# Transformer block on one core: row sums taken with the last projection, squares and normalizing on ScalarE, and modulation of two tiles at once

## The chip, the cores and the metric

The kernel runs on one core of one Trainium2 chip. The metric is the device time of one execution in microseconds (us), the median of several runs of the same program. A profile of one execution, taken by the hardware profiler, goes with it. Engine names are those of the profile: PE (TensorE, matmuls), DVE (VectorE), ACT (ScalarE), POOL (GpSimd), SP (SyncE, which only issues transfers here).

## The reference

```python
h = _layernorm(x, axis=-1) * (1 + ca) + sa
x = x + ga * attention(h)          # 16 heads, softmax over the query axis
h = _layernorm(x, axis=-1) * (1 + cb) + sb
x = x + gb * ffn(h)                # fp4 blocks: w_down(silu(w_gate h) * (w_up h))
```

x is (2, 2048, 256) in float32. The six rows ca to gb come from a small product of c with wmod and are the same for all rows of a batch. In the feed-forward part (256 to 704 and back) the activations, h and the hidden product, are rounded to a grid of fp4 values in blocks of 16 with a scale of their own; the weights as well. The layer norm is `(x - mean) / sqrt(var + 1e-5)` over the 256 numbers of a row.

## The kernel before

**Tiles.** A tile is 128 rows of x, one row per partition, 256 numbers long. A batch has 16 tiles, in four groups of four. The attention of both batches takes the greater part of the time, and the feed-forward of the first batch is spread between the attention steps of the second. For the second (last) batch nothing is left to hide behind, so that its last projection and its feed-forward stand at the end, as a tail with functions of its own.

**Order of work.** Every piece of work is a Python generator (a chain) with a due time. The class `Order` plans: it keeps a clock for each engine, estimates each operation, and emits whatever can start first, due times deciding between candidates. What comes out is one fixed list of instructions for each engine, executed in that order; an instruction that has to wait holds back all behind it on its engine. Buffers are counted as "rooms": three places `s` of two PSUM banks each, two single banks `o`, five `e` buffers, two `ln`, and so on. A chain that takes a room waits until an earlier owner gives it back.

**The tail, as the change finds it.** `project_last` multiplies the attention output of the last four heads with the output projection, tile by tile, into PSUM: tiles 0 to 3, 4 to 7 and 8 to 11 into `s` places (`op_0`, `op_4`, `op_8`), tiles 12, 13 and 14, 15 into the two `o` banks (`op_12`, `op_14`). `projected` brings the result into x. For tiles 0 to 7 VectorE adds it to x. For tiles 8 to 15 (`ADD_X = 2`, in groups of four) x itself has been added in PSUM, by one more matmul with the identity, and ScalarE or VectorE copies the sum out. `ffn_stats` takes mean and variance of each row with `bn_stats` and `bn_aggr` (in `ln_stats`), then an inverse root by three Newton steps on tiny operands; it handles tile 0, tiles 1 to 3, and then four tiles at a time. `tail_norm` makes h with two VectorE operations per tile, `(x - mean) * (1 + cb)` and `h * r + sb`, for tile 0, tile 1, and then pairs, and quantizes the result (`quantize`, ten small or large steps, of which `MAGIC` goes to ScalarE and the last product to GpSimd or VectorE). `tail` then does one tile: transpose of h (`hq`, into an `o` bank), a copy by ScalarE, the two products `pg` and `pu` (8 rows of the trace each), silu on ScalarE, product and quantizing on VectorE (tile `e`), transpose (`h2t`), copy by ScalarE, and `dn`: x by the identity, then six products with the down weights. Tile 15 is done in two halves. In names below, `pg_3` is the product of tile 3, and so on.

Two things about `project_last` matter for the change: the matmul that writes a further part of a PSUM place waits until the part before it has been read, and `hq_0`, the first transpose of the tail, takes the `o` bank that `op_12` used.

Of the kernel before, what the change touches and what calls it, by code (L numbers as in the profile page):

```python
# [10 lines left out]
F32 = mybir.dt.float32  # L11
# [3 lines left out]
AF = mybir.ActivationFunctionType  # L15
ALU = mybir.AluOpType
# [4 lines left out]
P = 128  # L21
EPS = 1e-5
# [22 lines left out]
TAIL_MARGIN = 0.5  # L45
# [2 lines left out]

PROJECT_DUE = -0.5, 0.0, 0.2, 0.4
PROJECTED = (0, 4), (4, 4), (8, 4), (12, 2), (14, 2)  # L50
ADD_X = 2
NORM_DUE = -0.4, -0.2, 0.6
STATS_LEAD = 4
NORM_LEAD = 3.5
LAST_LEAD = 0.5
SPLIT = 1
# [54 lines left out]
class Order:  # L111
# [23 lines left out]
    def signal(self, key, of=1, early=0.0):  # L135

        n, t = self.counts.get(key, (0, 0.0))
        n, t = n + 1, max(t, self.chain.end - early)
        self.counts[key] = (n, t)
        if n == of:  # L140
            self.done[key] = t
        return n == of

    def give(self, name, n=1, place=0):
        for _ in range(n):
            heapq.heappush(self.rooms[name], (self.chain.end, place))
# [188 lines left out]
def adaln_block(  # L335
# [15 lines left out]
    B, N, D = x_in.shape  # L351
# [3 lines left out]
    I = w_gate.shape[0]  # L355
    KC = D // P
    NT = N // P
# [17 lines left out]
    T, V, A, G, S = (  # L375
        Queue(n, e)
        for n, e in (
            ("PE", nc.tensor),
            ("DVE", nc.vector),
            ("ACT", nc.scalar),  # L380
            ("POOL", nc.gpsimd),
            ("SP", nc.sync),
        )
# [4 lines left out]
            h=2, qm=2, h2=2, h2t=1, hqt=1, st=1, qs=3, ln=2,  # L388
# [4 lines left out]
    signal, give, due = order.signal, order.give, order.due  # L393

    const = ctx.enter_context(tc.tile_pool(name="const", bufs=1))
# [8 lines left out]
    vp = ctx.enter_context(tc.tile_pool(name="vp", bufs=5))  # L404
    w2 = ctx.enter_context(tc.tile_pool(name="w2", bufs=2))
    small = ctx.enter_context(tc.tile_pool(name="small", bufs=6))

    def banks(place, name):

        return ps_s.tile([P, 2, 512], F32, tag=f"s{place}", name=name)  # L410
# [7 lines left out]
    def either(first, second, margin):  # L418
        return Best(first, second, margin=COPY_MARGIN if margin is None else margin)

    def copy(dst, src, margin=None):
        return either(A.copy(dst, src), V.tensor_copy(dst, src), margin)

    def matmuls(dst, pairs, first=True):
        return [
            T.matmul(dst, lhsT=l, rhs=r, start=(first and k == 0), stop=(k == len(pairs) - 1))
            for k, (l, r) in enumerate(pairs)
        ]
# [22 lines left out]
    def x_tile(b, t):  # L451
        return xs[b, t // 4][:, t % 4, :]
# [6 lines left out]
    def mod(b, which):  # L459
        return mods[:, b, MODS.index(which), :]  # L460
# [31 lines left out]
    ident = const.tile([P, P], F32, tag="ident", name="ident")  # L492
# [78 lines left out]
        signal("mods")  # L571


    def ln_stats(x4, name, centre=False):


        n = x4.shape[1]
        yield Wait(take=["ln"])
        mv = small.tile([P, 4, 2], F32, tag="mv", name=f"mv{name}", bufs=2)
        for t in range(n):  # L580
            st = small.tile([P, 6], F32, tag="bst", name=f"st{name}_{t}")
            yield Free(V.bn_stats(st, x4[:, t, :]))
            yield V.bn_aggr(mv[:, t, :], st)
        v, r, e, c = (
            small.tile([P, 4], F32, tag=f"ln{i}", name=f"ln{i}{name}", bufs=2)[:, 0:n]
            for i in range(4)
        )
        yield V.tensor_scalar(v, mv[:, 0:n, 1], EPS, None, ALU.add)

        yield V.tensor_scalar(r.bitcast(U32), v.bitcast(U32), 1, None, ALU.logical_shift_right)  # L590
        yield V.tensor_scalar(
            r.bitcast(I32), r.bitcast(I32), -1.0, float(0x5F3759DF), ALU.mult, ALU.add
        )
        for i in range(3):
            yield V.tensor_tensor(e, r, r, ALU.mult)
            yield V.scalar_tensor_tensor(e, e, -0.5, v, ALU.mult, ALU.mult)
            if i < 2:
                yield V.scalar_tensor_tensor(r, e, 1.5, r, ALU.add, ALU.mult)
        yield V.scalar_tensor_tensor(e, e, 0.5, r, ALU.add, ALU.mult)
        yield V.tensor_tensor(r, r, e, ALU.add)  # L600
        if centre:
            return mv[:, :, 0], r
        yield V.scalar_tensor_tensor(c, mv[:, 0:n, 0], -1.0, r, ALU.mult, ALU.mult)
        return c, r

    def pool(*args, margin):
        if margin is None:
# [598 lines left out]
    def project_last(b, q, t, n):  # L1206

        g = t // 4
        room = "s" if n > 2 else "o"
        (place,) = yield Wait(  # L1210
            [("osb", b, q, g), ("wo", b, q), ("x", b, g)]
            + [("out", b, q - 1, t + j) for j in range(n)],
            [room],
        )
        name = f"op{b}_{q}_{t}"
        if room == "s":
            ps = banks(place, name)
        else:
            ps = ps_o.tile([P, 512], F32, tag="o", name=name).unsqueeze(1)
        taken = [1, 1, 2] if t == 0 else [2] * (n // 2)  # L1220
        for k, m in enumerate(taken):
            first = sum(taken[:k])
            part = ps[:, first // 2, first % 2 * D : (first % 2 + m) * D]
            for j in range(m):
                u = t + first + j
                pairs = [
                    (o_sb[b, 2 * q + c][:, u * P : (u + 1) * P], wos[b, q][:, c, :])
                    for c in range(2)
                ]
                if g >= ADD_X:  # L1230
                    pairs = [(ident, x_tile(b, u))] + pairs
                yield Free(matmuls(part[:, j * D : (j + 1) * D], pairs))
            order.add(
                projected(b, q, t + first, m, part, order.chain.end, (room, place, t, len(taken))),
                order.chain.due,
            )

    def projected(b, q, t, n, ps, ready, where):

        room, place, first, parts = where  # L1240
        order.chain.base = ready + order.CROSS
        x2 = xs[b, t // 4][:, t % 4 : t % 4 + n, :]
        ps = ps.rearrange("p (j d) -> p j d", d=D)
        if t // 4 >= ADD_X:
            yield copy(x2, ps, TAIL_MARGIN)
        else:
            yield V.tensor_tensor(x2, ps, x2, ALU.add)
        if signal(("projected", b, q, first), of=parts):
            give(room, place=place)
        for j in range(n):  # L1250
            signal(("out", b, q, t + j))

    def load_x(b, g):
        yield Wait(take=["x"])
# [3 lines left out]


    lns = {}  # L1260

    def lns_of(t):

        return t - t % 4 if t > 3 else min(t, 1)

    def ffn_stats(b, t, n):
        yield Wait([("out", b, NQUAD - 1, t + j) for j in range(n)])
        x4 = xs[b, t // 4][:, t % 4 : t % 4 + n, :]
        c, r = yield from ln_stats(x4, f"f{b}_{t}", centre=b == B - 1)
        for j in range(n):  # L1270
            lns[b, t + j] = (c, r, j, n)
        signal(("ln", b, t))
# [73 lines left out]
        give("h2t")  # L1346


    tails = {}

    def silu_table():
        yield Wait([("w", len(steps) - 1, 0)])
        yield A.activation(sig[:, :, 0], sig[:, :, 0], AF.Silu)
# [18 lines left out]
    def residual(ps, b, t):  # L1372
        return T.matmul(ps[:, 0:D], lhsT=ident, rhs=x_tile(b, t), start=True, stop=False)

    def tail_norm(b, t, n):

        margin = 0.0 if t < 2 else TAIL_MARGIN
        yield Wait([("ln", b, lns_of(t))], ["v"])
        w = vp.tile([P, 2, 2, D], F32, tag="v", name=f"w{b}_{t}")
        for j in range(n):  # L1380
            mean, r, k, of = lns[b, t + j]
            h, x = w[:, 0, j, :], x_tile(b, t + j)
            yield Free(
                V.scalar_tensor_tensor(
                    h, x, mean[:, k : k + 1], mod(b, "cb"), ALU.subtract, ALU.mult
                )
            )
            signal(("centred", b, t + j))
        for j in range(n):
            mean, r, k, of = lns[b, t + j]  # L1390
            h = w[:, 0, j, :]
            yield Wait([("centred", b, t + j)])
            yield Free(
                V.scalar_tensor_tensor(h, h, r[:, k : k + 1], mod(b, "sb"), ALU.mult, ALU.add)
            )
            if signal(("applied", b, t + j - k), of=of):
                give("ln")
        h, m = (w[:, i, 0:n].rearrange("p j d -> p (j d)") for i in range(2))
        yield from quantize(h, n * D // BLK, f"h{b}_{t}", m, margin)
        for j in range(n):  # L1400
            tails[b, t + j] = (w, j, n)
            signal(("normed", b, t + j))
# [138 lines left out]
    for b in range(B):  # L1541
# [28 lines left out]
        else:  # L1570
# [5 lines left out]
            for t in (0, 1, *range(2, NT, 2)):  # L1576
                if t < 4:
                    dues = d + NORM_DUE[(t + 1) // 2]
                else:
                    dues = d + t - STATS_LEAD  # L1580
                if t == lns_of(t):
                    add(ffn_stats(b, t, (1, 3)[t] if t < 4 else 4), dues)
                add(tail_norm(b, t, 1 if t < 2 else 2), dues if t < 4 else d + t - NORM_LEAD)
            for t in range(NT):
# [49 lines left out]
```

## Time and profile before

| | us |
|---|---|
| median of 3 runs | 1929.37 (1929.2 to 1930.44) |
| the profiled execution's own time | 1929.38 |
| its span in the trace | 1927.6 |
| PE busy | 1898.0 (98%) |
| DVE busy | 1711.0 (89%) |
| ACT busy | 1317.7 (68%) |
| POOL busy | 617.2 (32%) |
| first projection matmul of the tail | 1749.25 |
| first `pg` matmul of the tail | 1770.40 |
| last matmuls (`dn` of tile 15) | 1922.83 |

Times inside the trace count from the start of the span. The granted clock of PE was full. All operations are recorded by one helper, so that every row has the same line (L273), and one reads by the tile names. A duration in a row includes some overlap with the next row on the same engine: what an operation costs its queue is the distance from one start to the next. The trace shows each float32 matmul as two rows.

### The profile page before, as it was taken

The numbers are of one execution on the slowest core, as the hardware profiler recorded it, in microseconds if no ns is written. First come the engines' busy times: TensorE is split into PE (matmuls) and PEld (weight loads), VectorE is DVE, ScalarE is ACT, GpSimd is POOL, SyncE is SP. The second block draws the span as 40 slices with busy tenths as digits, with TensorE's granted clock in tenths as the row PEclk, the third lists the DMA queues.
The fourth block names the chain that finished last, engine by engine and source line by source line (L and its number), as shares of the span: only waits on it lengthen the run. The fifth ranks groups of instructions, "written<-read, shape, count | busy, mean of one in ns | idle before, by whom it ended". The sixth has DMA issues, their size and how long they took to land.

```text
span 1927.6 us, 30282 instructions
## 1 busy us (share of the span) xinstructions
PE 1898.0 (98%) x10212; PEld 787.2 (41%) x10212; DVE 1711.0 (89%) x4170; ACT 1317.7 (68%) x1428; POOL 617.2 (32%) x1387
## 2 busy tenths in 40 slices
PE   9999999999999999999999999999999999999998
PEld 5333433343334333343334434334434343335666
DVE  5999999999999998888888788887888888997997
ACT  4787677777776676777777667676676777884333
POOL 0333333333443331113444344444443211230010
PEclk9999999999999999999999999999999999999999
DMA  6422121202120223211102210211011111100000
GB/s 211 100 67 55 38 56 50 47 19 49 46 62 4 50 55 94 77 39 45 52 16 61 64 44 18 55 36 39 9 37 44 34 34 34 39 1 1 12 17 17
DMA packets 40395, 88.02 MB, mean 46 GB/s; under 512 B 6320, under 2 KB 22576, under 8 KB 36272
## 3 DMA queue, kind: packets, MB, share of 16 engines
q1 hardware_dynamic: 38880, 83.98, 16.9%
q8 instruction: 82, 1.34, 0.3%
q10 hardware_dynamic: 1360, 2.10, 0.3%
q14 instruction: 73, 0.60, 0.1%
HBM read 63.51 MB, written 20.97 MB: 44 GB/s over the span
## 4 chain that ended last, share of the span: by engine, by line
PE 84%; DVE 13%; ACT 2%; issue 1%; POOL 0%; ACTq 0%; POOLq 0%; DVEq 0%
PE o L273 43%; PE ps L273 15%; DVE e L273 8%; PE op L273 6%; PE v L273 6%; PE dn L273 3%; PE qk L273 2%; PE up L273 2%; PE gate L273 2%; PE h2t L273 1%; DVE w L273 1%; PE pg L273 1%; PE pu L273 1%; ACT e L273 1%; PE busy L273 1%
## 5 line engine op out<-in xcount | busy, mean ns | idle before, releaser
L273 DVE TENSOR_SCALAR_CACHE_REDUCE e<-ps 128x1024 f32<-128x1024 f32 x1024 | 1226.1, 1215 | 90.5 <-PE ps L273 65.6
L273 ACT ACTIVATE e<-e,mn 128x2048 f32<-128x2048 f32 x512 | 1025.2, 2002 | 393.1 <-POOL mn L273 391.3
L273 PE MATMUL o<-e,vn 128*64 128x512 f32 x4096 | 993.4, 603 | 5.9 <-ACT osb L273 2.2
L273 PEld LDWEIGHTS o<-e,vn 128*64 128x64 f32 x4096 | 255.0, 136 | 454.1 <-issue 371.4
L273 POOL TENSOR_SCALAR mn<-mn 128x1 f32<-128x1 f32 x512 | 152.3, 298 | 731.4 <-DVE rz L273 285.3
L273 PE MATMUL ps<-q,k 64*128 64x512 f32 x2048 | 371.4, 445 | 2.2 <-DVE e L273 1.7
L273 PEld LDWEIGHTS ps<-q,k 64*128 64x128 f32 x2048 | 159.7, 184 | 346.6 <-DVE e L273 116.4
L273 POOL TENSOR_SCALAR vn<-v,rz 128x64 f32<-128x64 f32 x512 | 165.5, 323 | 309.2 <-DVE rz L273 217.4
L273 PE MATMUL op<-wo,osb 128*64 128x256 f32 (+1 forms) x960 | 125.3, 382 | 2.5 <-DVE x L273 1.8
L273 PE MATMUL v<-wv,ht 128*64 128x256 f32 x1024 | 124.0, 381 | 0.9 <-DVE st L273 0.6
L273 DVE RECIPROCAL rz<-z 128x1 f32<-128x1 f32 x512 | 80.3, 157 | 26.5 <-ACT e L273 25.5
L273 PEld LDWEIGHTS op<-wo,osb 128*64 128x64 f32 (+1 forms) x960 | 74.3, 140 | 61.1 <-issue 22.6
L273 PEld LDWEIGHTS v<-wv,ht 128*64 128x64 f32 x1024 | 71.3, 137 | 65.0 <-issue 26.9
L273 ACT ACTIVATION_READ_ACCUMULATOR e<-e,mn 128x1 f32 x512 | 95.4, 186 | 0.0
L273 DVE DVE_READ_ACCUMULATOR e<-ps 128x1 f32 x1024 | 84.2, 82 | 0.0
L273 ACT COPY osb<-o 64x512 f32<-64x512 f32 x104 | 60.2, 579 | 23.6 <-PE o L273 21.7
L273 PE MATMUL qk<-ht,wqk_sb 128*64 128x512 f32 (+1 forms) x224 | 61.7, 598 | 0.9 <-ACT ht L273 0.9
L273 POOL TENSOR_TENSOR h<-h,m 128x704 f32<-128x704 f32 x32 | 54.1, 1689 | 12.6 <-DVE m L273 7.9
L273 DVE TENSOR_TENSOR x<-op,x 128x512 f32<-128x512 f32 (+1 forms) x61 | 41.2, 676 | 13.7 <-PE op L273 13.3
L273 PE MATMUL dn<-wdb,e 117*128 117x256 f32 (+1 forms) x192 | 45.1, 382 | 3.3 <-ACT e L273 3.1
L273 ACT ACT_TABLE_LOAD x34 | 43.6, 1283 | 4.3 <-issue 3.7
L273 PE MATMUL dn<-wd_t,h2t 117*64 117x256 f32 (+1 forms) x384 | 45.8, 381 | 0.0
(243 smaller groups left out, 1454.8 us busy)
## 6 DMA issues: line engine op xcount, KB each, us to landing
k<-scr SPq DMA_DIRECT2D x124, 256.0 KB, 4.6
scr<-st SPq DMA_DIRECT2D x32, 512.0 KB, 3.2
q<-scr SPq DMA_DIRECT2D x124, 128.0 KB, 5.6
x<-in_x_dram SPq DMA_DIRECT2D x8, 512.0 KB, 4.4
wv<-in_wv_dram SPq DMA_DIRECT2D x8, 256.0 KB, 3.7
wo<-in_wo_dram SPq DMA_DIRECT2D x8, 256.0 KB, 2.7
xt<-in_x_dram SPq DMA_DIRECT2D x4, 512.0 KB, 7.2
out_dram<-h2t SPq DMA_DIRECT2D x16, 128.0 KB, 1.8
```

What stands on the lines that cost most here:

```text
L273: op = Op(self.name, *self.estimate(method, args, kw, lambda: f(*args, **kw)))
```

## The change

The adds of the last projection become sixteen VectorE operations, one per tile, which also give the sum of each row (`accum_out`); the identity matmuls of tiles 8 to 15 and the ScalarE copies go. The sum divided by 256 is the mean. ScalarE squares `mean - x` and sums the squares, for all 16 tiles, into `squares`; the values themselves go to a scratch tile, `unread`. The inverse root is as before (`inverse_root`). Tiles 0 to 3 are still made by the two VectorE operations per tile (now `centre`). For tiles 4 to 15 (`BY_SCALAR = 4`) ScalarE normalizes, `r * x - r * mean`, and VectorE multiplies with `1 + cb` and adds `sb` for two tiles in one operation each. The helpers `ln_tiles` and `inverse_root` are parts of the old `ln_stats`. All that the kernel does before the tail is in the same order in both programs.

```diff
-ADD_X = 2
+BY_SCALAR = 4
...
+    def inverse_root(v, r, e):
...
                     for c in range(2)
                 ]
-                if g >= ADD_X:
-                    pairs = [(ident, x_tile(b, u))] + pairs
                 yield Free(matmuls(part[:, j * D : (j + 1) * D], pairs))
...
-        if t // 4 >= ADD_X:
-            yield copy(x2, ps, TAIL_MARGIN)
-        else:
-            yield V.tensor_tensor(x2, ps, x2, ALU.add)
+        for j in range(n):
+            yield Free(
+                V.scalar_tensor_tensor(
+                    x2[:, j, :],
+                    ps[:, j, :],
+                    1.0,
+                    x2[:, j, :],
+                    ALU.mult,
+                    ALU.add,
+                    accum_out=sums[:, t + j : t + j + 1],
+                )
+            )
+            signal(("out", b, q, t + j))
         if signal(("projected", b, q, first), of=parts):
             give(room, place=place)
-        for j in range(n):
-            signal(("out", b, q, t + j))
...
+    sums = const.tile([P, NT], F32, tag="sums", name="sums")
+    squares = const.tile([P, NT], F32, tag="squares", name="squares")
...
-        c, r = yield from ln_stats(x4, f"f{b}_{t}", centre=b == B - 1)
+        if b < B - 1:
+            c, r = yield from ln_stats(x4, f"f{b}_{t}")
+        else:
+            c = sums[:, t : t + n]
+            yield V.tensor_scalar(c, c, 1.0 / D, None, ALU.mult)
+            yield Wait(take=["ln"])
+            if "unread" not in tails:
+                yield Wait(take=["qm"])
+                tails["unread"] = w2.tile([P, I], F32, tag="qm", name="unread")[:, 0:D]
+            for j in range(n):
+                op = A.activation(
+                    tails["unread"],
+                    x4[:, j, :],
+                    AF.Square,
+                    bias=c[:, j : j + 1],
+                    scale=-1.0,
+                    accum_out=squares[:, t + j : t + j + 1],
+                )
+                yield Free(op) if j else op
+            v, r, e, k = ln_tiles(n, f"f{b}_{t}")
+            yield V.tensor_scalar(v, squares[:, t : t + n], 1.0 / D, EPS, ALU.mult, ALU.add)
+            yield from inverse_root(v, r, e)
+            if t >= BY_SCALAR:
+                yield V.scalar_tensor_tensor(k, c, -1.0, r, ALU.mult, ALU.mult)
+                c = k
...
+        if t >= BY_SCALAR:
+            for j in range(n):
+                c, r, k, of = lns[b, t + j]
+                yield Free(
+                    A.activation(
+                        w[:, 0, j, :],
+                        x_tile(b, t + j),
+                        AF.Identity,
+                        bias=c[:, k : k + 1],
+                        scale=r[:, k : k + 1],
+                    )
+                )
+                if signal(("applied", b, t + j - k), of=of):
+                    give("ln")
+            for which, op in (("cb", ALU.mult), ("sb", ALU.add)):
+                h = w[:, 0, 0:n, :]
+                yield V.tensor_tensor(
+                    h, h, mod(b, which).unsqueeze(1).to_broadcast([P, n, D]), op
+                )
+        else:
+            yield from centre(b, t, n, w)
```

More of the change, by code (lines that the diff above doesn't have):

```diff
@@ L571, in mod_rows, with ln_stats @@
         signal("mods")
-    def ln_stats(x4, name, centre=False):
+    def ln_stats(x4, name):
         n = x4.shape[1]
@@ L583, in ln_stats, with ln_tiles @@
             yield V.bn_aggr(mv[:, t, :], st)
-        v, r, e, c = (
+        v, r, e, c = ln_tiles(n, name)
+        yield V.tensor_scalar(v, mv[:, 0:n, 1], EPS, None, ALU.add)
+        yield from inverse_root(v, r, e)
+        yield V.scalar_tensor_tensor(c, mv[:, 0:n, 0], -1.0, r, ALU.mult, ALU.mult)
+        return c, r
+    def ln_tiles(n, name):
+        return [
             small.tile([P, 4], F32, tag=f"ln{i}", name=f"ln{i}{name}", bufs=2)[:, 0:n]
             for i in range(4)
-        )
-        yield V.tensor_scalar(v, mv[:, 0:n, 1], EPS, None, ALU.add)
+        ]
+    def inverse_root(v, r, e):
         yield V.tensor_scalar(r.bitcast(U32), v.bitcast(U32), 1, None, ALU.logical_shift_right)
@@ L600, in ln_stats @@
         yield V.tensor_tensor(r, r, e, ALU.add)
[L601 to L604, printed above, removed]
     def pool(*args, margin):
@@ L1260, in adaln_block @@
     lns = {}
+    tails = {}
+    sums = const.tile([P, NT], F32, tag="sums", name="sums")
+    squares = const.tile([P, NT], F32, tag="squares", name="squares")
     def lns_of(t):
@@ L1268, in ffn_stats @@
         x4 = xs[b, t // 4][:, t % 4 : t % 4 + n, :]
-        c, r = yield from ln_stats(x4, f"f{b}_{t}", centre=b == B - 1)
+        if b < B - 1:
[19 more added lines that the diff above has]
+            yield V.tensor_scalar(v, squares[:, t : t + n], 1.0 / D, EPS, ALU.mult, ALU.add)
+            yield from inverse_root(v, r, e)
+            if t >= BY_SCALAR:
+                yield V.scalar_tensor_tensor(k, c, -1.0, r, ALU.mult, ALU.mult)
+                c = k
         for j in range(n):
@@ L1346, in ffn @@
         give("h2t")
-    tails = {}
     def silu_table():
@@ L1373, in residual, with centre @@
         return T.matmul(ps[:, 0:D], lhsT=ident, rhs=x_tile(b, t), start=True, stop=False)
[L1375 to L1379, printed above, removed]
+    def centre(b, t, n, w):
         for j in range(n):
@@ L1397, in tail_norm @@
                 give("ln")
+    def tail_norm(b, t, n):
+        margin = 0.0 if t < 2 else TAIL_MARGIN
+        yield Wait([("ln", b, lns_of(t))], ["v"])
+        w = vp.tile([P, 2, 2, D], F32, tag="v", name=f"w{b}_{t}")
+        if t >= BY_SCALAR:
[19 more added lines that the diff above has]
+            yield from centre(b, t, n, w)
         h, m = (w[:, i, 0:n].rearrange("p j d -> p (j d)") for i in range(2))
```

## The prediction

> **What bounds the kernel now.** Only the tail is touched (the two built programs are the same up to the first projection matmul at 1749.25), so I read the tail alone, first by stage: busy time of each engine in five stretches (PE, weight loads, DVE, ACT, POOL, then clock and DMA).
>
> ```profile
> 1749.00:1770.40 21.40, 18.91 (x84) 15.15 (x83) 16.95 (x84) 5.97 (x11) 0.00 (x0) 1.00 0.01 1
> 1770.40:1800.00 29.60, 27.95 (x106) 18.47 (x105) 28.30 (x91) 10.40 (x18) 3.65 (x3) 1.00 0.02 5
> 1800.00:1840.00 40.00, 36.84 (x160) 26.39 (x159) 37.30 (x104) 13.47 (x23) 2.61 (x2) 1.00 0.04 14
> 1840.00:1880.00 40.00, 37.57 (x163) 27.74 (x162) 39.99 (x119) 14.64 (x25) 3.65 (x3) 1.00 0.05 17
> 1880.00:1927.60 47.60, 41.27 (x182) 30.21 (x180) 34.10 (x86) 15.56 (x27) 3.75 (x3) 0.98 0.05 18
> ```
>
> PE and DVE are both nearly full; ACT (60 of 179 us) and POOL are not. Next, whom PE waited for from 1749 on (sum, times, longest):
>
> ```profile
> PE pg L273 <- ACT w L273: 3.9, 9, 0.8
> PE dn L273 <- ACT e L273: 3.1, 6, 0.6
> PE hq L273 <- POOL w L273: 2.6, 4, 1.0
> PE op L273 <- DVE x L273: 1.8, 3, 0.8
> PE op L273 <- ACT x L273: 0.7, 1, 0.7
> PE h2t L273 <- DVE e L273: 0.6, 1, 0.6
> ```
>
> After `pg_0` PE loses 10.2 us. The first two lines are the copy between a transpose and the matmul that needs it, 0.5 each (0.3 where two transposes stand together). The third is VectorE being late with a pair of h. Last, the chain of waits at the beginning of the tail:
>
> ```profile
> 1757.91 5.03 PE op L273 x22
> 1762.96 0.59 ACT x L273
> 1763.60 5.45 PE op L273 x24
> 1769.05 0.22 PE hq L273 x2
> 1769.27 1.30 PE op L273 x6
> 1770.57 2.37 PE pg L273 x8
> ```
>
> The fill is PE's: projection matmuls one after another until `pg_0` (PE's own timeline has it at 1770.40). VectorE had h of tile 0 ready at 1766.1 (last product at 1765.66). From `pg_0` to the end at 1924.4 PE carries 154 us of work and waits.
>
> [...] the Relu of that shape takes 0.51 here. [...] so that two tiles at once save the fixed part alone. The trace agrees: start to start 0.60 for 512, 0.34 for 256. [...] The new add has one source in PSUM; nothing here shows it with a sum. [...] the product at 1888.49 took 1.63 instead of 0.88 while POOL ran. [...]
>
> **The change part by part.** The view by shapes has the costs (count, busy sum and mean ns):
>
> ```profile
> L273 DVE SCALAR_TENSOR_TENSOR w<-x,mvf,mods 128x256 f32<-128x256 f32 x16 | 7.6, 475 | 0.0
> L273 DVE SCALAR_TENSOR_TENSOR w<-w,ln1f,mods 128x256 f32<-128x256 f32 x16 | 7.4, 475 | 0.0
> L273 DVE BATCH_NORM_STATS2 stf<-x 128x6 f32<-128x256 f32 x16 | 6.6, 414 | 0.0
> ...
> L273 DVE BATCH_NORM_AGGREGATE mvf<-stf 128x2 f32<-128x6 f32 x16 | 2.8, 172 | 0.0
> ```
>
> Rows overlap by some 75 ns, so I price by start to start in the DVE timeline: pointer operation 0.40, `bn_stats` 0.34, `bn_aggr` 0.09, tiny operations 0.085 when something stands between dependent ones.
>
> *VectorE, whole tail.* Off: 16 x 0.34 + 16 x 0.09 for the statistics, adds 2 x 0.34 + 3 x 0.60, pointer operations of 12 tiles 24 x 0.40: 19.0. On: 16 adds with sum. The score pass with a minimum (1024 wide) goes 1.15 start to start, its accumulator read of 0.08 included, which leaves next to nothing for the read. I take 0.36; the bounds are 0.34 (the plain add) and 0.60 (halved). 16 x 0.36, 12 modulations x 0.60, 8 tiny ones: 13.6. Net -5.4. The last product of `e` moves between POOL and VectorE for a few tiles, 0.35 in all.
>
> *PE.* Eight identity matmuls, 16 rows at 0.217: 3.5 off, all inside the fill.
>
> *ScalarE.* Four copies of 0.585 off; 16 squares of 0.51 + 0.19 (the read after an exponential takes 186 ns) and 12 normalizings of 0.59 on: +16 us, into an engine idle for 119. Only its order can hurt. The built order has one table load in the tail, as before. SP's queue is the same; no DMA moves.
>
> *The fill.* Here the gain is not collected. `hq_0` needs the `o` bank of `op_12`. Before, a ScalarE copy freed it; now it is VectorE's 14th add, and in the built order w_0, w_1 to its exponent mask and half of w_2 stand ahead of it. The adds at 1751.28, 1752.93, 1754.58 and 1757.17 each wait for matmuls that have not changed, so the count starts at 1757.17. From there to that 14th add: 10 adds x 0.36 = 3.6; 8 pointer operations = 3.2; reduces 2 x 0.34 + 0.60 = 1.3; 3 products 1.0; 2 masks 0.3; 2 rounding steps 0.7; 3 reciprocals 0.6; 39 tiny ones 3.3: 14.0. Waits for PE within it: each part of `op_4` and `op_8` is written only after the part before it is read, and read only after the next tile is written; tile 7 ends at 1759.2, tiles 8 to 10 at 1761.8, tile 11 at 1763.3, against VectorE at 1759.0, 1761.1 and 1762.4: 0.25 + 0.75 + 0.9 = 1.9. So the add ends at 1757.2 + 14.0 + 1.9 = 1773.1. PE has been through with the projection since 1766.9 and idles. `hq_0` to its `pg` takes 0.90 (as 1775.14 to 1776.04): `pg_0` at 1774.1, **3.7 later**. Bounds: no waits for PE, +1.8; adds at 0.60, +6.1. The squares hide: tile 0's ends about 1753.3, when VectorE is waiting for the third tile's matmul; the others have 3 us of adds over them.
>
> *After `pg_0`.* In the built PE order there are 4 single and 4 double transposes right ahead of their `pg` (4 x 0.52 + 4 x 0.29 = 3.2), 6 `h2t` with only the identity product between them and their `dn` (3.1), and tile 15's last two waits (1.2): 7.5 instead of 10.2. The POOL waits go: VectorE has 5.4 us less, and most of its new work is done before `pg_0`. Each wait also costs some 0.16 of unoverlapped matmul end (`dn` 2.86 after a wait, 2.70 to the next start), and there are four fewer: -0.6. Against it, ScalarE's order: the Relu of w_8 stands behind the copy of `h2t_5`, and that of e_10 behind the copy of `hq_12`, so that VectorE waits for them. None to 3 us; I take 1.0. Net **-2.3**.
>
> *The end* keeps its shape: the Relu of tile 15's second half still stands behind the copy of its first half.
>
> **Sum.** 3.7 - 2.3 = +1.4. The profiled execution took 1929.38 (span 1927.6 and 1.8 around it), the median is 1929.37: **1930.8**.
>
> **Rivals.** *Slower:* ScalarE's queue takes VectorE's place. Relus and copies wait behind squares, normalizings and copies whose matmuls are not done; then POOL is late with pairs as before. The 2.3 is not collected and the fill's 3.7 stays: 1933.1; with two more waits of 0.9, 1934.9. For it: 24 more operations in an in-order queue, several ahead of a copy that PE waits for. Against it: ACT idles two thirds of the tail today. It decides from 2.5 us of such waits on, PE's pg and dn lines together above 9. *Faster:* the fill costs nothing, because VectorE gets through its adds without waits, tiny operations hiding under PE; then `pg_0` comes at 1770.4 or before, and -3.3 from the middle gives 1926.1; if PE's 3.5 counted too, 1922.6. For it: PE is the bound of the fill today. Against it: 14.0 us of VectorE work after 1757.17 are there whoever waits. It needs the 14th add before 1769.5. *The sum is slow:* adds at 0.60 put the fill at +6.1: 1933.2. That the squares need another table is excluded by the built order.
>
> **How the numbers follow.** A measurement of this kernel can tell about 0.2%, 3.9 us, from no change. My forecast (about 1927 to 1933 by its bounds) has 0.5, the slower rival 0.25, the slow sum 0.05, the faster rival 0.2. Half of each slower case lies beyond 1933.2, and the forecast's own tail adds to it: slower 0.3, faster 0.2, same 0.5. The range, 1925.0 to 1935.0, leaves out the far ends of both.
>
> **What would show it.** `hq_0` near 1773 behind a wait for a VectorE add, PE idle for some 6 us ahead of it; no or few `hq` waits for POOL; 154 us from `pg_0` to the end shrunk to some 151.7; adds of 0.36 start to start; ACT at about 76 us in the tail. A `pg_0` before 1771.5 would prove the fill wrong; pg and dn waits above 9 us the middle.

## The result, and the profile after

| | before | after |
|---|---|---|
| median, us | 1929.30 (8 runs, 1929.13 to 1930.60) | 1935.91 (8 runs, 1934.42 to 1936.74) |
| ratio to before, 95% interval | | 1.0031 (1.0023 to 1.0040) |
| span of the profiled execution | 1927.6 | 1933.6 |
| first add of the tail to `pg_0` | 19.12 | 23.13 |
| `pg_0` to `pu_0` | 2.37 | 4.57 |
| `pu_0` to the last `dn` | 150.06 | 149.88 |

The kernel became 6.6 us slower; the forecast was 1930.8, with a range to 1935.0. The rows inside the trace are counted from the first VectorE add of the last projection (1751.28 and 1751.25), because the tail starts at slightly different times in different executions of the same beginning: from 1750.73 to 1752.55 in the runs below. They account for 6.03 us: 4.01 until `pg_0` (the fill, as it is called below), 2.20 inside `pg_0`, -0.18 in all that follows. The remaining 0.6 is no part of these rows: the profiled execution of the kernel after took 1935.37, 0.5 less than its median. Executions of one and the same program differ by 1.2 us (e15 below) to 5.8 us (e8), so that differences between medians of a microsecond or two are read here from the traces.

The kernel after by stages (PE, weight loads, DVE, ACT, POOL, then clock and DMA):

```profile
1749.00:1766.90 17.90, 15.37 (x66) 11.75 (x64) 10.82 (x71) 8.51 (x23) 0.00 (x0) 1.00 0.01 2
1766.90:1773.10 6.20, 0.00 (x0) 0.00 (x0) 6.20 (x32) 0.51 (x1) 0.00 (x0) 0.90 0.00 0
1773.10:1779.00 5.90, 5.31 (x11) 3.06 (x12) 4.93 (x24) 1.64 (x4) 0.85 (x1) 0.53 0.00 0
1779.00:1800.00 21.00, 20.24 (x78) 13.47 (x77) 17.57 (x47) 9.98 (x20) 1.27 (x2) 1.00 0.00 1
1800.00:1840.00 40.00, 37.77 (x167) 27.84 (x165) 37.59 (x101) 18.76 (x37) 3.83 (x3) 1.00 0.05 17
1840.00:1880.00 40.00, 36.37 (x154) 26.01 (x155) 37.61 (x101) 16.11 (x27) 5.20 (x4) 1.00 0.04 14
1880.00:1933.60 53.60, 46.55 (x204) 33.99 (x202) 39.19 (x100) 17.40 (x31) 2.57 (x2) 0.99 0.05 18
```

The second row is new: 6.2 us in which PE does nothing and VectorE is busy all the time. The third row is what I had not thought of: PE works again, but the column of the granted clock says 0.53. PE's own timeline before, from `hq_0` to `pu_0` (rows of `op` in between left out):

```profile
1768.89 0.38 PE L273 MATMUL hq<-ident,w 128*128 128x128 f32 x2
...
1770.40 2.53 PE L273 MATMUL pg<-wg_t,w 128*128 128x352 f32 x8
1772.77 2.53 PE L273 MATMUL pu<-wu_t,w 128*128 128x352 f32 x8
```

And after, with the start of VectorE's 14th add below the dots:

```profile
1763.70 3.19 PE L273 MATMUL op<-wo,osb 128*128 128x256 f32 x14
1773.17 0.69 PE L273 MATMUL hq<-ident,w 128*128 128x128 f32 x2 [6.29 <-DVE x L273]
1774.38 4.74 PE L273 MATMUL pg<-wg_t,w 128*128 128x352 f32 x8 [0.52 <-ACT w L273]
1778.95 2.53 PE L273 MATMUL pu<-wu_t,w 128*128 128x352 f32 x8
...
1772.70 0.41 DVE L273 SCALAR_TENSOR_TENSOR x<-op,x 128x256 f32<-128x256 f32 x1
```

Eight rows of `pg_0` take 4.74 and the eight of `pu_0`, of the same shape, 2.53; two transposes take 0.69 instead of 0.38. `hq_0` waited 6.29 us for an add of x, the one that frees the bank of `op_12`. Whom PE waited for from 1749 on (sum, times, longest; two lines under a microsecond left out):

```profile
PE hq L273 <- DVE x L273: 6.3, 1, 6.3
PE dn L273 <- ACT e L273: 4.1, 7, 0.8
PE pg L273 <- ACT w L273: 3.7, 9, 0.5
PE op L273 <- DVE x L273: 2.0, 3, 0.9
PE h2t L273 <- DVE e L273: 1.3, 2, 0.7
PE hq L273 <- POOL w L273: 1.1, 1, 1.1
```

Without the first line and `op` the waits sum to 11.0, against 10.2 before: POOL's 2.6 fell to 1.1, and `dn` and `h2t` took more than the difference. The new operations in the view by shapes (count, busy sum and mean ns):

```profile
L273 DVE TENSOR_TENSOR w<-w,mods 128x512 f32<-128x512 f32 x12 | 8.2, 684 | 0.3 <-ACT w L273 0.3
L273 DVE SCALAR_TENSOR_TENSOR x<-op,x 128x256 f32<-128x256 f32 x16 | 6.6, 418 | 9.7 <-PE op L273 9.7
L273 ACT ACTIVATE w<-x,ln3f,ln1f 128x256 f32<-128x256 f32 x12 | 6.5, 592 | 0.0
L273 ACT ACTIVATION_READ_ACCUMULATOR unread<-x,sums 128x1 f32 x16 | 3.0, 187 | 0.0
```

They cost what they were priced at: the add with a sum 0.35 from start to start (1754.56 to 1754.91), where the plain add before took 0.34 (1752.93 to 1753.27), both with one source in PSUM; the normalizing with two pointers 0.59 (592 ns in the view), for which before had no row; the read after a square 0.19; each of the modulations 0.68 or 0.69 with its overlap, 0.60 from start to start (1783.31 to 1783.91). None of them ran while GpSimd did. The prices of the operations were not the error.

### The profile page after: what moved, and what is told of

It reads as the page before. It is cut to its first block, busy times and chain, and to the rows that moved or that the text cites. A ratio compares the mean times of both kernels' runs of the same rounds, so it can differ in the third digit from the quotient of the medians.

```text
span 1933.6 us, 30287 instructions
## 1 busy us (share of the span) xinstructions
PE 1897.0 (98%) x10196; PEld 785.2 (41%) x10196; DVE 1708.3 (88%) x4161; ACT 1330.7 (69%) x1468; POOL 617.2 (32%) x1387
## 4 chain that ended last, share of the span: by engine, by line
PE 85%; DVE 12%; ACT 2%; issue 1%; POOL 0%; ACTq 0%; POOLq 0%; DVEq 0%
PE o L273 42%; PE ps L273 15%; DVE e L273 7%; PE v L273 6%; PE op L273 5%; PE dn L273 4%; PE qk L273 2%; PE pg L273 2%; PE up L273 2%; PE gate L273 2%; PE pu L273 2%; PE h2t L273 1%; ACT e L273 1%; PE busy L273 1%; DVE w L273 0%
## 5 line engine op out<-in xcount | busy, mean ns | idle before, releaser
L273 PE MATMUL pg<-wg_t,w 128*128 128x352 f32 x128 | 44.0, 485 | 3.7 <-ACT w L273 3.7
```

The costliest lines, as they stand in the source:

```text
L273: op = Op(self.name, *self.estimate(method, args, kw, lambda: f(*args, **kw)))
```

## The experiments

All times inside the trace are from the first add; "hq_1 to end" runs from the start of `hq_1` to that of the last `dn` row. The last two columns come from one traced execution of each kernel, the times are medians.

| kernel | us | ratio to before | first add to hq_1 | hq_1 to end |
|---|---|---|---|---|
| before | 1929.3 | 1 | 23.86 | 147.69 |
| after | 1935.91 | 1.0031 (1.0023 to 1.0040) | 30.06 | 147.52 |
| e1_fill24 | 1936.62 | 1.0039 (1.0027 to 1.0052) | 31.56 | 147.52 |
| e2_fill14 | 1932.85 | 1.0020 (1.0012 to 1.0029) | 27.72 | 147.51 |
| e3_adds_early | 1934.13 | 1.0029 (1.0017 to 1.0040) | 25.56 | 150.50 |
| e4_norm_only | 1930.32 | 1.0005 (0.9996 to 1.0013) | 23.85 | 148.79 |
| e5_half_adds | 1926.43 | 0.9986 (0.9980 to 0.9993) | 23.08 | 145.48 |
| e6_adds_alone | 1940.50 | 1.0055 (1.0043 to 1.0068) | 32.64 | 149.21 |
| e7_norm_vector | 1932.35 | 1.0011 (1.0005 to 1.0018) | 30.92 | 143.97 |
| e8_gpsimd_adds | 1941.18 | 1.0063 (1.0049 to 1.0077) | 28.76 | 156.08 |
| e9_half_vector | 1929.81 | 1.0003 (0.9994 to 1.0011) | 23.09 | 148.92 |
| e10_three_quarters_vector | 1932.23 | 1.0015 (1.0008 to 1.0021) | 23.71 | 150.83 |
| e11_three_quarters | 1934.38 | 1.0024 (1.0015 to 1.0034) | 23.71 | 151.72 |
| e12_lead_4 | 1934.58 | 1.0025 (1.0015 to 1.0035) | 30.09 | 145.94 |
| e13_stats_lead_3 | 1942.09 | 1.0066 (1.0053 to 1.0079) | 26.34 | 155.25 |
| e14_half_lead_4 | 1929.76 | 1.0000 (0.9992 to 1.0008) | 23.09 | 149.14 |
| e15_half_stats_lead_3 | 1935.09 | 1.0030 (1.0018 to 1.0043) | 24.03 | 154.32 |

### PE's clock: e1_fill24 and e2_fill14

```diff
...
+        if t == 0:
+            fill = banks(order.rooms["s"][0][1], "fill")[:, 0, 0:D]
+
+            def filler():
+                for _ in range(24):          # e2: 14
+                    nc.tensor.matmul(fill, lhsT=ident, rhs=mods[:, 0, 0, :], start=True, stop=True)
+
+            ops = [Op("PE", 0.0, filler, mode=ops[0].mode)] + ops
+        yield ops
```

> The kernel after, with 24 matmuls of the identity by a modulation row (about 24 x 0.217 = 5.2 us, their result is never read) ahead of hq_0 on PE, so that PE idles 0.5 to 1.1 us there instead of 6.3; the order of everything else is the same. Theory that the idle time slows PE's clock: hq_0 still at 1773.2, its two transposes 0.38 instead of 0.69, pg_0 2.5 instead of 4.74, pu_0 some 2.3 to 2.6 earlier, time 1933.4 (1933.0 to 1933.8). Rival, that the first pg is slow for another reason (its weights, a bank): pg_0 stays at 4.7 and the time at 1935.9.

> As the run with 24, with 14 matmuls (3.0 us): the idle time ahead of hq_0 shrinks to 3.2 us. The traces so far show no slowing after 1.1 us of idle time and one after 6.3. If 3.2 us is short enough, pg_0 takes 2.5 and the time is 1933.4 as with 24; if not, pg_0 takes 4.7 and the time stays at 1935.9; something between if the slowing is gradual.

I had sized the filler wrongly: 0.217 is the price of one row, and each of these matmuls is two rows (x28 below for 14). So 24 matmuls took 10.5 us and held `hq_0` up by 3.9 us, and the 14 of e2 took 6.1 us and closed the gap almost exactly. Neither run has the 3.2 us gap that e2 was meant to have. PE's timeline in e2 (`pu_0` follows at 1776.08):

```profile
1766.20 6.21 PE L1477 MATMUL fill<-mods,ident 128*128 128x256 f32 x28
1772.66 0.44 PE L273 MATMUL hq<-ident,w 128*128 128x128 f32 x2 [0.25 <-DVE x L273]
1773.61 2.63 PE L273 MATMUL pg<-wg_t,w 128*128 128x352 f32 x8 [0.52 <-ACT w L273]
```

`hq_0` starts as long after the first add as in the kernel after (21.93 and 21.92). `pg_0` now takes 2.63, `pu_0` comes 2.35 us earlier counted from the first add, and the time is 3.1 us lower (the rest does not lie between the first add and the last `dn`). Useless work on PE makes this kernel faster, with the same weights in the same bank, which rules out the rival that one of these is slow. Even e1, whose `hq_0` is 3.9 us later than after, reaches `hq_1` only 1.5 us later, since its `pg_0` is fast.

The column of the granted clock shows the slow stretch as well. The kernel after reads 0.50 from 1774 to 1778 and 1.00 from 1779 to 1780, with `pu_0` beginning at 1778.95, 5.8 us after `hq_0`. e6 below has this stretch, with 0.50 in that column too:

```profile
1776.00:1780.00 4.00, 3.22 (x7) 1.82 (x8) 3.93 (x16) 0.56 (x2) 1.06 (x1) 0.50 0.00 0
```

In the tails of these kernels every idle time from 2.48 us on was followed by slow matmuls (2.48, 2.51, 2.70, 2.92, 2.99, 3.11, 3.22, 3.26 and more). Of the shorter ones, one was. It is in e8:

```profile
1839.28 2.86 PE L274 MATMUL dn<-wdb,e 117*128 117x256 f32 x12 [0.50 <-ACT e L274]
1843.83 0.84 PE L274 MATMUL h2t<-ident,e 128*118 128x128 f32 x6 [1.68 <-DVE e L274]
...
1845.61 4.52 PE L274 MATMUL dn<-wdb,e 117*128 117x256 f32 x12 [0.51 <-ACT e L274]
```

The same twelve rows of `dn` take 2.86 and then 4.52. An idle time of 1.76 in e8 and those of 1.90 and 1.92 in e11 had no such effect. So below 2.5 us the length of one gap does not decide alone; what does, no run here shows.

### What bounds the fill: e3, e6, e5, e8

e3_adds_early, in the kernel after:

```diff
             order.add(
                 projected(b, q, t + first, m, part, order.chain.end, (room, place, t, len(taken))),
-                order.chain.due,
+                order.chain.due - 0.6,
```

> The kernel after, with every add due 0.6 steps earlier, so that in the built order the four adds of tiles 12 to 15 stand ahead of w_1 and w_2 on VectorE. Theory of the fill (the bank of op_12 holds hq_0 up, and the long idle time slows pg_0): hq_0 then waits for h of tile 0, about 1768.1; pg_0 at 1769.3, 2.5 long, pu_0 at 1771.8 instead of 1778.95; if the rest keeps its 149.9 from pu_0 to the last dn, time 1928.8 (1927 to 1930.5). Rival, that another wait comes in its place (tile 0's own chain pushed back by the adds, or pairs late afterwards): pg_0 after 1771 or the rest above 152, time 1931 to 1934.

The rival held, in its second form: from `pu_0` to the last `dn` it took 156.3 us instead of 149.9. `pg_0` came at 17.30 after the first add, 5.83 earlier than in the kernel after, and was fast. But the adds had been moved ahead of tile 1's chain, and the same idle time turned up one tile later, with the same slow `pg`:

```profile
1776.60 0.41 PE L273 MATMUL hq<-ident,w 128*128 128x128 f32 x2 [3.26 <-DVE q_h L273]
1777.52 4.33 PE L273 MATMUL pg<-wg_t,w 128*128 128x352 f32 x8 [0.51 <-ACT w L273]
```

The bank of `op_12` is thus only the place where the lateness shows. What is late is VectorE as a whole: its adds and the norms of the first tiles are more than PE's work covers. In the orders that were tried with all these adds on VectorE, `hq_0` waits (after, e12) or `hq_1` does (e3, and e13 below with 3.65 us).

e6_adds_alone, in the kernel before:

```diff
-ADD_X = 2
+ADD_X = 4
```

> The kernel before with one constant changed, so that all 16 tiles are added on VectorE (plain adds of two tiles, 4 more of 0.60), without identity matmuls and ScalarE copies; statistics and normalizing as before. PE loses 3.5 us. Theory that VectorE's work bounds the fill: in the built order op_12's add stands behind the last product of w_1, so hq_0 comes later than in the kernel after, about 1775 to 1777, PE idles 8 to 10 us, the first pg takes 4.7; time 1936 to 1940. Rival, that PE bounds the fill: pg_0 at 1767 to 1768, time 1926 to 1927.

```profile
1776.26 0.69 PE L273 MATMUL hq<-ident,w 128*128 128x128 f32 x2 [9.07 <-DVE x L273]
1777.47 5.06 PE L273 MATMUL pg<-wg_t,w 128*128 128x352 f32 x8 [0.52 <-ACT w L273]
1782.32 3.00 PE L273 MATMUL pu<-wu_t,w 128*128 128x352 f32 x8
```

One constant, and the kernel is 11.2 us slower than before, though PE has 3.5 us less to do: 9.07 us of idle time, then a clock of 0.50 until into `pu_0` (0.50 from 1780 to 1783, 0.98 from 1783 to 1790; expected were 8 to 10 us and a time of 1936 to 1940; it is 1940.5). By its own kernels the change falls into three steps: all adds to VectorE +11.2 (before to e6), sums and squares in place of `bn_stats` -8.2 (e6 to e7, next section), normalizing on ScalarE +3.6 (e7 to after). Only the first is mainly the fill (8.8 us until `hq_1`); the other two lie mostly after `hq_1`, and what such differences are worth is the question of the last two groups of experiments.

e5_half_adds gives tiles 8 to 15 back their identity matmul, copy and `bn_stats`, and keeps the rest of the change (line numbers differ by one):

```diff
+ADD_X = 2
...
+                if g >= ADD_X:
+                    pairs = [(ident, x_tile(b, u))] + pairs
...
+        if t // 4 >= ADD_X:
+            yield copy(x2, ps, TAIL_MARGIN)
+            for j in range(n):
+                signal(("out", b, q, t + j))
-        for j in range(n):
+        for j in range(n if t // 4 < ADD_X else 0):
...
-        if b < B - 1:
+        if b < B - 1 or t // 4 >= ADD_X:
             c, r = yield from ln_stats(x4, f"f{b}_{t}")
```

> The kernel after, with tiles 8 to 15 as before: x by the identity on PE, a ScalarE copy of two tiles, statistics by bn_stats; ScalarE's normalizing stays. Theory that the whole loss arises in the fill, from the eight adds that VectorE was given there: hq_0's bank is free early again, PE is not idle for more than 1.1 us ahead of it, pg_0 at 1770.4 (PE's own end of the fill, 3.5 us of identity matmuls included) and 2.5 long, pu_0 at 1772.8; with 149.9 from there the time is 1929.2 (1928 to 1931). Rival, that the sums and squares of tiles 0 to 7 or the normalizing carry part of the loss: pu_0 later than 1773.5, or the rest above 151.5, 1931 to 1934.

```profile
1769.38 0.38 PE L274 MATMUL hq<-ident,w 128*128 128x128 f32 x2
...
1770.90 2.53 PE L274 MATMUL pg<-wg_t,w 128*128 128x352 f32 x8
```

No wait ahead of `hq_0` or `pg_0`, and no slow matmul. Until `hq_1` it takes 6.98 us less than the kernel after, and 0.78 less than before. At 1926.43 it is the fastest kernel of the study, below its forecast too: 2.0 us come from the stretch after `hq_1`, which the theory of the fill had left alone.

e8_gpsimd_adds tried to relieve both engines (the copies go to a buffer, GpSimd adds):

```diff
+ADD_X = 2
...
+        if t // 4 >= ADD_X:
...
+            y = w2.tile([P, I], F32, tag="qm", name=f"y{b}_{t}")
+            y2 = y[:, 0 : n * D].rearrange("p (j d) -> p j d", d=D)
+            yield A.copy(y2, ps)
...
+            yield G.tensor_tensor(x2, x2, y2, ALU.add)
...
-        if b < B - 1:
+        if b < B - 1 or t // 4 >= ADD_X:
```

> The kernel after, with tiles 8 to 15 added by neither PE nor VectorE: ScalarE copies two tiles of the projection from PSUM to a buffer (0.6 each), GpSimd adds x (512 wide, about 1.5 each by its product of that width), statistics by bn_stats later. PE has no identity matmuls, VectorE has eight adds less in the fill. If VectorE's work and PE's identity matmuls are the two bounds of the fill, both shrink: h of tile 0 about 1764.5, PE through the projection about 1765.5, pg_0 1766 to 1768 and 2.5 long, time 1925.5 (1924 to 1928). Rival, that GpSimd is late or slows VectorE down by contention, or that the third pair comes late and PE idles over 3 us again: 1929 to 1933.

Both parts of the rival came, VectorE slowed down while GpSimd ran and idle times of PE (3.11 and 2.48 us), and cost far more than its 1929 to 1933: the time is 1941.18. VectorE stood still for 2.55 us, because ScalarE's squares of tiles 4 to 7 stood behind a copy that waited for PE. Then three of VectorE's operations ran against GpSimd's three adds (3.89 us from 1765.20 on):

```profile
1765.63 1.13 DVE L274 SCALAR_TENSOR_TENSOR w<-w 128x256 f32<-128x256 f32 x1 [0.34 <-ACT w L274]
1766.68 1.22 DVE L274 SCALAR_TENSOR_TENSOR ln2f<-ln2f,ln0f 128x3 f32<-128x3 f32 x1
1767.89 1.49 DVE L274 SCALAR_TENSOR_TENSOR w<-w 128x256 f32<-128x256 f32 x1
```

They cost 0.42, 0.16 and 0.42 alone. The one with three numbers per row took 1.06 us longer, those with 256 took 0.71 and 1.07 longer, so the delay did not go with the size; what causes it, the trace does not show. Until `hq_1` e8 loses 4.9 us to before; the larger part of its loss, 8.4, lies after it.

### The stretch after hq_1: e4, e7, e9, e10, e11

The first theory for the 2.3 us that were not collected was ScalarE's order. In four pairs of kernels the edit changes only who normalizes tiles 4 to 15. (The planner answers each edit with a plan of its own, and more than the order changes in it; see the next section.)

e4_norm_only is before with the new branch of `tail_norm` for tiles 4 to 15 (`bn_stats` stays, and gives `c` and `r`).

> The kernel before with one part of the change alone: for tiles 4 to 15 ScalarE normalizes and VectorE modulates two tiles at once; adds, identity matmuls, statistics and copies are as before, and so is the fill (pg_0 at 1770.4). VectorE loses 24 x 0.40 - 12 x 0.60 = 2.4 us, ScalarE gains 12 x 0.59 = 7.1. Theory that ScalarE's order gives the gain of VectorE away again: time 1929.3 to 1931, PE's waits for copies (pg, dn) above the 7.0 of before while those for POOL shrink. Rival, that normalizing on ScalarE pays and the squares and adds spoil it: 1926.5 to 1927.5.

e7_norm_vector is after with one constant changed:

```diff
-BY_SCALAR = 4
+BY_SCALAR = 16
```

> The kernel after, with all 16 tiles normalized by VectorE as in before (24 x 0.40 instead of 12 x 0.60, so 2.4 us more for VectorE and 7.1 less for ScalarE); adds with sums and squares stay. The fill is nearly the same (in the built order the 14th add stands where it stood): pg_0 1774 and 4.7 long. Theory that ScalarE's order costs the 2 to 3 us that the middle lost: from pu_0 to the last dn 147 to 148.5, time 1933 to 1934.5. Rival, that the middle is set by PE and by where the planner puts things, and ScalarE's normalizing weighs nothing: 149 to 151, time 1935 to 1937.

e9_half_vector is e5 with that constant (and `ln_stats` gives the mean again where VectorE normalizes); e10 and e11 are e9 and e5 with `ADD_X = 3`.

> The kernel of e5_half_adds with all tiles normalized by VectorE (the third pair of kernels that differ in that alone). The fill is the same, pg_0 at 1770.9. Theory that ScalarE's normalizing is what costs the middle (3.5 us from hq_1 to the last dn between the kernel after and e7_norm_vector): hq_1 to the last dn 142 to 144.5 instead of 145.5, time 1923 to 1925.5. Rival, that 3.5 us was chance of that one order: 145 to 148, time 1926 to 1929.

> The kernel of e9_half_vector with tiles 8 to 11 added on VectorE too: PE loses 8 identity rows (1.74 us) in the fill, VectorE gains 4 adds with sum (1.4 us) ahead of h of tile 0; op_12, whose bank hq_0 takes, stays with ScalarE's copy. If both bounds stand near each other in the fill, pg_0 comes at 1769.0 to 1769.8 with PE idle less than 2 us and 2.5 long, and hq_1 waits less than 1 us: time 1 to 1.5 below e9_half_vector. Rival, that h of tile 0 or 1 is late by more than that: pg_0 after 1770.9 or a wait over 2.5 us ahead of hq_1 with a slow pg: as e9_half_vector or up to 3 us above it.

> The kernel of e5_half_adds with tiles 8 to 11 added on VectorE too, ScalarE normalizing as there (fourth pair with e10_three_quarters_vector). The same fill as that one; theory that ScalarE's normalizing costs the middle: 1 to 4 us above e10_three_quarters_vector. Rival, chance of the order: within 1 us of it, or below.

| normalized by | VectorE | ScalarE | difference |
|---|---|---|---|
| before / e4 | 147.69 | 148.79 | +1.10 |
| e7 / after | 143.97 | 147.52 | +3.55 |
| e9 / e5 | 148.92 | 145.48 | -3.44 |
| e10 / e11 | 150.83 | 151.72 | +0.89 |

By the times of e4 and e7 the theory looked proven. But e4's own trace spoke against it: the waits for copies (`pg` and `dn`), which the theory wanted above 7.0, fell to 4.7, and POOL's to 0.7. What e4 lost sits in one wait, for a product of `e` that stood late in VectorE's own queue, with slow matmuls behind it:

```profile
1836.73 1.51 PE L273 MATMUL h2t<-ident,e 128*118 128x128 f32 x6 [4.10 <-DVE e L273]
```

The third pair turned the theory round, at the same size (e9 was expected at 1923 to 1925.5, by the rival at 1926 to 1929). In e9 the planner also gave VectorE three more of the last products of `e` than in e5, 0.88 us each, so that this pair is not a clean one either. Neither ScalarE's normalizing nor VectorE's saving decides this stretch alone, and my theory of ScalarE's queue fell. By its median e11 is 2.15 us above e10, within the theory's 1 to 4, but the stretch accounts for 0.9 of it. e10 and e11 also missed in the fill: the adds of tiles 8 to 11 made `hq_0` and `hq_1` wait 0.5 and 0.7 for h, and `hq_1` came 0.6 later than in e5 and e9.

### Nearly the same work in another plan: e12 to e15

```diff
-NORM_LEAD = 3.5
+NORM_LEAD = 4.0      # e12 (on after), e14 (on e5)
```

e13 (on after) and e15 (on e5) take `STATS_LEAD = 3` for 4 and `NORM_LEAD = 2.5`. The source asks for the same work. But the planner writes more than an order: it also chooses between GpSimd and VectorE for the last product of `e` (0.88 us on VectorE). GpSimd makes it for 4 whole tiles in after, 5 in e12 and 6 in e13, for 5 tiles and a half one in e5, 3 in e14 and 2 in e15.

> The kernel after with one number of the planner changed: the norms of tiles 4 to 15 are due 4.0 instead of 3.5 steps ahead of their tile. The same matmuls, the same ScalarE operations; in the built order nothing changes up to the first quantizing of e_0, so the fill is the same (pg_0 at 1774.4, slow). Theory that the middle is set by where the planner's order puts PE's waits and not by what the operations cost: hq_1 to the last dn differs from the 147.5 of after by over 1.5 us, either way. Rival, that the cost of the work sets it (ScalarE's normalizing, VectorE's sum): 146.5 to 148.5, time 1935 to 1937.

> The kernel after with two numbers of the planner changed: statistics of tiles 4 to 15 due 3 instead of 4 steps ahead, norms 2.5 instead of 3.5. The same work; a few tiny operations and the squares of tiles 4 to 7 leave the fill, so that pg_0 may come up to 1 us earlier, slow all the same. Theory of the order: hq_1 to the last dn away from 147.5 by over 1.5 us. Rival, that the work sets it: 146.5 to 148.5.

> The kernel of e5_half_adds with the norms due 4.0 instead of 3.5 steps ahead; the same fill (pg_0 at 1770.9). Theory of the order: hq_1 to the last dn (145.5 in e5) anywhere from 144 to 151.7, what the orders so far spanned, most likely longer than 145.5, since e5's is the second shortest: time 1925 to 1932. Rival, that the work sets it: 144.5 to 146.5, time 1925.5 to 1927.5.

> The kernel of e5_half_adds with statistics due 3 and norms 2.5 steps ahead. As e14: by the theory of the order 144 to 151.7 from hq_1 to the last dn, by the rival 144.5 to 146.5; in the fill pg_0 stays at 1770.9, since PE bounds it there.

All four left 147.5 or 145.5 by more than 1.5 us: to 145.94 (by 1.58, just beyond the mark) and 155.25 with the kernel after, to 149.14 and 154.32 with that of e5. e15 is even beyond the 151.7 that its expectation allowed. Two misses lie in the fill: e13's `pg_0` came 5.4 us earlier than in after, where at most 1 was expected, and was fast (`hq_1` then waited 3.65 us in its place); e15's `pg_0` came 0.95 later than in e5, where it should have stayed.

One plan repeats well: after, e1 and e2 have the same one after `hq_1`, the same operations on the same engines, and took 147.52, 147.52 and 147.51. So the differences belong to the plans, though not every plan is as steady: the 13 executions of e14 go from 1927.25 to 1931.25, and the trace is of the slowest. Whether the order or the division of the last products weighs more is not separated. The three shortest stretches (e5, e7, e12) are the three plans with five whole tiles on GpSimd, which speaks for the division; but six and seven (e13, e3) took 155.25 and 150.50, so more on GpSimd is not simply better. e14 shows how 3.7 us come together, a pair of h that GpSimd delivers late and the slow `pg` behind it:

```profile
1877.34 0.66 PE L274 MATMUL hq<-ident,w 128*128 128x128 f32 x4 [2.51 <-POOL w L274]
1878.29 4.33 PE L274 MATMUL pg<-wg_t,w 128*128 128x352 f32 x8 [0.29 <-ACT w L274]
```

It costs e14 all that e5 had gained. The 0.78 us that e5 gains in the fill returned in e9 and e14, whose fill is the same, so it belongs to the edit (e15's other leads lose it); the 2.2 us after `hq_1` belong to the plan that e5 happened to get, and are luck. I did not look for a better plan still.

## Why the prediction was wrong, by its own steps

- **The fill, +3.7: right.** The 14th add was to end at 1773.1 and ended at 1773.12; `hq_0` near 1773, measured 1773.17; `pg_0` at 1774.1, measured 1774.38. Counted from the first add it is 4.01 later; the 0.3 beyond 3.7 are the slow transposes of `hq_0`. The three waits for PE inside it were put at 0.25, 0.75 and 0.9 and measured 0.22, 0.73 and 0.98. The idle time of "some 6 us" is there, with 6.29.
- **The first step that failed is a term put at nothing: what PE does after idling.** The prediction had the idle time in its sum and in its list of signs, but let `pg_0` run at its old price. e2 puts the omission at 2.35 us (`pu_0` earlier by that, nothing else moved). With it, the sum would have been 1933.2.
- **The second step that failed is the sum after `pg_0`, -2.3; measured -0.18.** The structural waits came as counted: `pg` 3.2 without that of `pg_0`, and six `dn`. The term "none to 3, I take 1.0" for new lateness measured about 3: waits after `pg_0` are 10.5 instead of 7.5. One is the Relu of w_8 behind the copy of `h2t_5`, named in advance: VectorE waits 1.19 for it at 1840.62, and `hq_8` 1.08 for the pair at 1843.97. The others (0.66 for `h2t`, 0.78 for a `dn` behind two copies, 0.4 more in the other `dn`) were not foreseen. Of the four fewer waits, worth -0.6, one came: there are 19 after `pg_0`, and there were 20. What failed is not the price list but the step from a list of waits in the built order to a saving: e12 to e15 show that this stretch moves by up to 8.8 us (e5 to e15) when nothing but two due times of the planner changes. Why this plan got these waits beyond the one of w_8 stays open.
- **The slower rival** (1933.1: the fill's 3.7 stays and nothing is collected) describes what happened, but for its cause. PE's `pg` and `dn` lines sum to 8.6, under the 9 from which it was to decide, and giving the normalizing back to VectorE shortened this stretch in three pairs and lengthened it in one. That ScalarE's queue is to blame isn't shown.
- **The faster rival** needed the 14th add before 1769.5. e3 meets that (its last add of all starts at 1767.74, and `pg_0` is earlier than before) and shows why it gains nothing: tile 1 is then late instead.
- **The slow sum** (adds at 0.60, an estimate of mine from the price of a 512-wide add before, 1754.58 to 1755.18) is out: 0.35. ACT's busy time in the tail is 72.9 where I had 76.
- **PE's 3.5 us** were not collected, as said. e6 has the same saving and loses 11.2.

## What to carry to other kernels

Before work is moved off the bounding engine of a stage, count the whole work of the engine that receives it up to the operation that lets the next stage start; here eight adds of 0.35 turned a stage bound by PE into one bound by VectorE. A gap on PE is to be priced with the slow matmuls behind it: in these tails 2.5 us or more of idle time cost some 1.4 to 3.2 us on top. Where a planner writes the order, not even the sign of a saving off the critical path is known before the change has been run in a second plan.

## What the runs showed of the hardware that I had not expected

Filling a gap on PE with 14 matmuls that nobody reads saved 3.1 us. What a gap costs on top follows its length only loosely: eight rows of `pg` took 4.33 instead of 2.53 or 2.63 after 2.51 and 3.26 us of idle time, but 4.92 after 2.99 (e15), 4.74 and 5.06 after 6.3 (after and e7), and 5.06 after 9.07. A gap of 1.68 us was once enough, one of 1.92 was not. A VectorE operation on 128x3 numbers took 1.22 us instead of 0.16 while GpSimd's adds ran (e8). And a fixed plan of 147.5 us repeated to 0.01 us in three traced executions.
